# Attention block on one core: VectorE's order in the projections, the place of the x loads, and when the second head pair gets its position terms

## The chip, the core and the metric

The kernel runs on one core of a Trainium2 chip. The metric is the device time of one execution in microseconds (us). The core has a matrix engine (TensorE, PE in the profile; its weight loads are PEld), two engines for elementwise work (VectorE, DVE; ScalarE, ACT), GpSimd (POOL) and SyncE (SP), which in this kernel issues most DMA transfers. Each engine works through its own list of instructions in order and waits on semaphores for the others. Matrix products land in PSUM, a small memory[...]; operands lie in SBUF.

## The reference, cut to what matters

Eight images of 512 channels and 32 x 32 pixels, all in float32:

```python
def cbs(x, w, p, pad): return silu(bn_eval(conv2d(x, w, pad), p))

def bot_attention(x, qkv_w, rw, rh):          # 4 heads of 64, 1024 pixels
    q, k, v = split(conv2d(x, qkv_w, 0))
    r = rw + rh                                # position terms, by column and by row
    logits = einsum('bhdi,bhdj->bhij', q, k + r) * HD ** -0.5
    return einsum('bhij,bhdj->bhdi', softmax(logits), v)

t = cbs(group_norm(x), cv1_w, cv1_bn, 0)       # 512 -> 512, 1x1
ys = [t[:, :256], t[:, 256:]]
for i in range(2):                             # two bottleneck units
    z = cbs(ys[-1], m_cv1_w[i], m_cv1_bn[i], 1)        # 3x3, 256 -> 256
    z = bot_attention(z, m_qkv_w[i], m_rw[i], m_rh[i])
    ys.append(ys[-1] + silu(bn_eval(conv2d(z, m_cv2_w[i], 0), m_cv2_bn[i])))
out = x + cbs(concatenate(ys, 1), cv2_w, cv2_bn, 0)    # 1024 -> 512, 1x1
```

## The kernel before, in words

Images go one after the other; `b` counts them from 0. An image has two units, `n` = 0 and 1. In each, TensorE's work comes in this order: the 3x3 convolution, the projections to q, k and v, attention, and the 1x1 convolution `m2` (lines 887 to 902). First convolutions of the next image (`cv1`) or parts of the output convolution (`strassen`, line 933) are put between.

The program is traced in this order, and a planner then lays out each engine's list. It takes instructions by their place in the program among those that it reckons to be ready, and it gives buffers out as it goes. `tc.issue_after(ins)` sets a bound: instructions traced in the block that run on the engine of `ins` come behind `ins` on that engine. It binds no other engine.

**The convolution (`conv3x3`, line 858).** It works on 4 x 4 output tiles in a transformed space. For each of two output halves `oc` there are three filter tiles `u` of 1 MB (three pairs of rows), and each gives 32 matmul instructions of 128 columns (line 872). ScalarE and VectorE bring each product back (`columns_out`, `rows_out`, lines 405 to 439); ScalarE applies silu. `rows_out` has two parts: `first`, when two of the three products are there, and `last`.

**Loads.** All large tiles of weights share a ring of five buffers of 1 MB: filters (`load_u`, line 309), the combined projection weights `sq` (`load_sq`, line 232), `w1` (line 115) and the output convolution's weights. From image 1 on, `u_of(n)` takes the first three filters as loaded earlier, loads the second three when the second half is traced, and then `sq`. The next image's x (four tiles of 512 KB, line 104) is loaded in the program after the first convolution; its buffers are those in which the output convolution of the image before keeps its results until they are stored (line 979). All these loads stand in SP's queue, each one behind what was queued before it. Stores and residual loads of the output convolution stand in POOL's queue.

**The projections (`project_strassen`, line 538).** In image 0 a plain form is used (`project`). In images 1 to 7, both units, z is seen as a 2 x 2 block matrix, channel half by pixel half, and seven block products stand in for eight. Each of them is a q, a k and a v part. PSUM has three buffers `ps_big` of two banks and one `ps_av` of two banks; the seven products go through them as `ps_a` to `ps_e`, `ps_w` and `ps_v`. VectorE forms the operand sums `t1` to `t4` (lines 582 and 591 to 593) and the results:

| Lines | What VectorE computes |
| --- | --- |
| 606, 607 | `u` = product c + product a (q and k, then v) |
| 608, 577, 578 | `k1` of the first channel half, then its position terms (`add_r(0, 1)`) |
| 610, 611 | `v1` and `q1` |
| 616 to 618 | `k2`, `q2`, `v2` from product d |
| 621 to 623 | `k3`, `q3`, `v3` |
| 624 to 626 | product e taken from `v2`, `k2`, `q2` |
| 577, 578, twice each | position terms of the second channel half (`add_r(1, half)`) |

Line 624 reads the bank `ps_v`, and lines 625 and 626 read `ps_e`; the buffers are free for attention after that. `t`, `u` and `m5` lie in the three SBUF buffers `pt`, which the convolution's input tiles use before and attention's exponentials use after.

**Attention (`attention_fast`, line 631).** There are four groups: a pair of heads (a channel half `c`) by a half of the 512-pixel query columns. A group has eight key blocks, taken two at a time: four pairs of steps per group, 16 per unit. In each pair TensorE computes two tiles of logits (line 656), ScalarE the exponentials into `pt` (line 660), VectorE adds them to `acc` for the softmax sum (lines 666 and 668), and TensorE multiplies with v one pair behind (line 682, into the single `ps_av` buffer). At a group's end ScalarE and VectorE move the result to `ao` (lines 689 and 690), after which the next group may use `ps_av`; TensorE sums `acc` over partitions (`s_ps`, line 700). The order of trace is in the loop at line 763: `behind.get(g)` hangs other work on the groups. In the first unit of all images but the last, that work is the next image's group normalisation: statistics of two x tiles (line 444) in the first group and of two in the second, then the rest, then `cv1`. In the second unit it is loads, and products of the output convolution behind the fourth group.

Of the kernel before, what the change touches and what calls it, by code (L numbers as in the profile page):

```python
# [47 lines left out]
ALU = mybir.AluOpType  # L48
# [13 lines left out]
def kernel(  # L62
# [16 lines left out]
    nc = tc.nc  # L79
    B, C1, HW = x.shape  # L80
    C2 = out.shape[1]
    N, C = m_cv1_w.shape[:2]
    F = m_rw.shape[2]
    NX = C1 // P
    NM = C // P
# [143 lines left out]

    def load_sq(n):  # L230
        w = ring([P, 4, 3, P], "sq")
        nc.sync.dma_start(w, sq_dram[n])
        return w

# [70 lines left out]
    def load_u(n, oc, i):  # L307
        u = new_u("u")
        nc.sync.dma_start(u, u_dram[n][oc][i])
        return u  # L310
# [13 lines left out]
    def stages(act, small, ps_big, ps_av, n_pt):  # L324
# [89 lines left out]
        def rows_out(dst, r12, r34, ends):  # L414


            sd = act.tile([P, 2, 2, NT * F], F32, tag="acc", name="sd", bufs=2)
            s_, d_, big_s, big_d = sd[:, 0, 0], sd[:, 0, 1], sd[:, 1, 0], sd[:, 1, 1]
            stt, tt = nc.vector.scalar_tensor_tensor, nc.vector.tensor_tensor

            def tiles(ap):
                return ap.rearrange("p (t w) -> p t w", w=F)

            def to(r):
                return dst.rearrange("p (t r w) -> p r t w", r=4, w=F)[:, r]

            def first():
                for i, rr in enumerate((r12, r34)):
                    tt(sd[:, i, 0], rr[:, 0], rr[:, 1], ALU.add)
                    tt(sd[:, i, 1], rr[:, 0], rr[:, 1], ALU.subtract)  # L430
                stt(to(1), tiles(big_d), -0.5, tiles(d_), ALU.mult, ALU.add)
                tt(to(2), tiles(s_), tiles(big_s), ALU.subtract)

            def last():
                stt(ends, ends, -6.0, sd[:, 0], ALU.mult, ALU.add)
                stt(to(0), tiles(big_s), -0.25, tiles(ends[:, 0]), ALU.mult, ALU.add)
                stt(to(3), tiles(big_d), -2.0, tiles(ends[:, 1]), ALU.mult, ALU.add)  # L437

            return first, last
# [95 lines left out]
                qk(c)  # L535
            return q, kr, vT

        def project_strassen(n, z, sq):


            q = act.tile([P, NM, HW], F32, tag="q", name="q")
# [28 lines left out]
            def v_of(ap):  # L570
                return ap.rearrange("p (j o) -> p j o", o=P)
# [7 lines left out]

            t = act.tile([P, 4, HALF], F32, tag="pt", name="t_z", bufs=n_pt)  # L580
            t1, t2, t3, t4 = (t[:, i] for i in range(4))
            tt(t1, b12, b11, ALU.subtract)
            ps_a, ps_b, ps_v = big(), big(), ps_av.tile([P, 2, HALF], F32, tag="av", name="pv_ps")
            u, m5 = kept("u_z"), kept("m5_z")
            product(ps_a, ps_v[:, 0], block_qkv(n, 0, 0), b11)
# [21 lines left out]
            tt(u[:, 2], ps_w[:, 0], u[:, 2], ALU.add)  # L607
            tt(k1, k1, u[:, 1], ALU.add)
            add_r(0, 1)
            tt(v1, v1, v_of(u[:, 2]), ALU.add)  # L610
            tt(q1, q1, u[:, 0], ALU.add)
            ps_d = big()
            product(ps_d, ps_w[:, 1], s3, t3)
            q2, k2, v2 = places(1, 0)
# [6 lines left out]
            tt(k3, k2, m5[:, 1], ALU.add)  # L621
            tt(q3, q2, m5[:, 0], ALU.add)
            tt(v3, v2, v_of(m5[:, 2]), ALU.add)
            tt(v2, v2, v_of(ps_v[:, 0]), ALU.subtract)
            tt(k2, k2, ps_e[:, 1], ALU.subtract)
            tt(q2, q2, ps_e[:, 0], ALU.subtract)  # L626
            for half in range(NH):
                add_r(1, half)
            return q, kr, vT

        def attention_fast(n, z, at, behind, sq=None):

            q, kr, vT = project(n, z) if sq is None else project_strassen(n, z, sq)
            behind.get(-1, lambda: None)()

            ao = act.tile([P, NM, HW], F32, tag="z", name="ao")
# [124 lines left out]
            for i in range(len(pairs) + 1):  # L763
                if i < len(pairs):
                    added = logits(pairs[i])
                    g, at_q = divmod(i, NQ)
                    with tc.issue_after(added.ins):
                        if at_q == NQ - 2 and g > 0:
                            rss[g - 1] = spread(g - 1, s_drams[g - 1])
                        if at_q == 0 and g > 1:  # L770
                            scale(g - 2, rss.pop(g - 2))
                if i > 0:
                    g, j0 = pairs[i - 1][0]
                    if j0 == 0 and g > 0:
                        s_drams[g - 1] = sums(g - 1)
                    times_v(pairs[i - 1])
                    if j0 == 0:
                        with tc.issue_after(added.ins):
                            behind.get(g, lambda: None)()
# [78 lines left out]
        def conv3x3(n, vs, u_of):  # L858
            z = act.tile([P, NM, HW], F32, tag="z", name="z")
            for oc in range(NM):  # L860
                us = u_of(oc)
                r = act.tile([P, 2, 2, NT * NW, 2], F32, tag="acc", name="r_mid", bufs=2)
                ends = act.tile([P, 2, NT * NW, 2], F32, tag="rs", name="r_ends", bufs=2)
                rs = (r[:, 0], r[:, 1], ends)
                flat = [a.rearrange("p r q o -> p r (q o)") for a in rs]
                first, last = rows_out(z[:, oc, :], *flat)
                for i in range(PAIRS):
                    ps = ps_big.tile([P, 2, NC, NT * NW], F32, tag="big", name="c3_ps")
                    for row in range(2):
                        for col in range(NC):  # L870
                            for k in range(NM):
                                nc.tensor.matmul(  # L872
                                    ps[:, row, col, :], us[i][:, k, row, SLOT[col], :], vs[i][:, k, row, col, :],
                                    start=(k == 0), stop=(k == NM - 1),
                                )
                    columns_out(rs[i], ps)
                    if i == 1:
                        first()
                last()
                for half in range(NH):  # L880
                    part = z[:, oc, ts(half, HALF)]
                    last_silu = silu(part, part, bn_m1[n] + oc)
            with tc.issue_after(last_silu.ins):
                table_of(AF.Exp)
            return z

        def m2(n, ao, yi, dst_of):

# [233 lines left out]
    for b in range(B):  # L1122
        more = b + 1 < B
        y1, y1n, y2 = ypad[b % 2], ypad[(b + 1) % 2], ypad[N]

        sq = {}

        def u_of(n):
            def of(oc):
                if b == 0 and oc == 1:  # L1130
                    if n == 0:
                        with tc.issue_after(last.ins):
                            for i in range(PAIRS):
                                make(n, oc, [i])
                    else:
                        for k in range(NM):
                            raws[n, oc, k] = load_raw(n, oc, k, "kv"[k])
                        with tc.issue_after(last.ins):
                            make(n, oc, [1])
                got = [us.pop((oc, i)) if (oc, i) in us else load_u(n, oc, i) for i in range(PAIRS)]  # L1140
                if b > 0 and oc == 1:
                    sq[n] = load_sq(n)
                return got

            return of


        z = s.conv3x3(0, vs, u_of(0))
        if b == 0:
            load_bottleneck(1)  # L1150
            raws[1, 0, 0] = load_raw(1, 0, 0, "y0", 2)
            raws[1, 0, 1] = load_raw(1, 0, 1, "pt", 3)
        if more:
            xs = [load_x(act, b + 1, c, NX) for c in range(NX)]


        parts = {}
# [37 lines left out]
        behind = {g: ahead for g in range(NG)} | {NG: first, NG + 1: second}  # L1195
        if b == 0:
            behind[-1] = lambda: make(1, 0, range(PAIRS))
        ao, check = s.attention_fast(0, z, b * N * NM * NH, behind, sq.get(0))
        last = s.m2(0, ao, y1, lambda oc, half: inner(y2, oc, half))
        if more:  # L1200
            s.cv1(w1, xs, nxt, y1n, Y0S)
# [5 lines left out]
        vs = s.tiles_in(y2)  # L1207
        with tc.issue_after(last.ins):
            check()
        z = s.conv3x3(1, vs, u_of(1))  # L1210
        w2 = ws = three = stored = None
        begun = {}
        if b == 0:
# [30 lines left out]
        behind = {1: ahead, NG: first, NG + 1: second}  # L1244
        if b == 0:
            behind |= {0: prepare, 2: lambda: make_sq(0), 3: lambda: make_sq(1)}
        ao, check = s.attention_fast(1, z, (b * N + 1) * NM * NH, behind, sq.get(1))
        ylast = act.tile([P, NM, HW], F32, tag="v", name="ylast")
        last = s.m2(1, ao, y2, lambda oc, half: ylast[:, oc, ts(half, HALF)])
        with tc.issue_after(last.ins):  # L1250
# [26 lines left out]
    with tc.If(held < P):  # L1277
        with ExitStack() as gs:
# [7 lines left out]
            with tc.For_i(0, B, 1) as b:  # L1286
                xts = [load_x(g_act, b, c, NX) for c in range(NX)]
                for _ in g.group_norm(xts):
                    pass
                g_y0 = g_act.tile([P, NM, HW], F32, tag="y0", name="y0")  # L1290
                g.cv1(load_w1(), xts, g_y0, ypad[0], range(2 * NM))
                yi = ypad[0]
                for n in range(N):
                    z = g.conv3x3(n, g.tiles_in(yi), lambda oc: [load_u(n, oc, i) for i in range(PAIRS)])
                    ao = g.attention_general(n, z)
                    if n + 1 < N:
                        g.m2(n, ao, yi, lambda oc, half: inner(ypad[N], oc, half))
                        yi = ypad[N]
                g_last = g_act.tile([P, NM, HW], F32, tag="v", name="ylast")
                g.m2(N - 1, ao, yi, lambda oc, half: g_last[:, oc, ts(half, HALF)])  # L1300
                g.cv2(b, load_w2(), (g_y0, ypad[0], ypad[N], g_last))
# [51 lines left out]
```

## Time and profile before

| | Before |
| --- | --- |
| Median of three runs | 2385.78 us |
| Range of the runs | 2382.54 to 2388.15 us |
| Profiled execution's own time | 2385.39 us |
| Its span in the trace | 2383.3 us |
| TensorE busy | 2326.4 us (98%) |
| VectorE busy | 1751.7 us (73%) |
| ScalarE busy | 947.7 us (40%) |
| Granted TensorE clock, mean | 0.998 |
| Bytes moved by DMA | 226.39 MB, mean 95 GB/s |

Times in the trace count from the span's start. A row of the timeline gives start, duration, engine, line, operation, output and inputs, and in brackets the idle time of the engine before it with what ended it. A row of the waits gives who waited for whom, the total in us, how often, and the longest. Matmuls are pipelined: a row's duration runs from the first start to the modelled end of the last, so that rows overlap.

### The profile page before, as it was taken

To read this page: it belongs to the slowest core of one execution; us is meant where nothing else is said; L and a number is where in the kernel's file an instruction comes from. 1 tells how busy PE (TensorE), PEld (TensorE's weight loads), DVE (VectorE), ACT (ScalarE), POOL (GpSimd) and SP (SyncE) were. 2 spreads that over 40 slices of the span, in tenths; PEclk is the share of its full clock that TensorE was granted. 3 is DMA by queue.
4 is the path that set the end of the run, shared out by engine and by line. 5 is a ranking of instruction groups with operands and counts; after the bars stand their busy time and mean duration, and the time that the engine had idled before them with its cause. 6 is when DMAs were issued, how large, how long until landed. Compare 5 with 4: busy or idle time off the path is not lost.

```text
span 2383.3 us, 36285 instructions
## 1 busy us (share of the span) xinstructions
PE 2326.4 (98%) x14794; PEld 1168.9 (49%) x14794; DVE 1751.7 (73%) x2811; ACT 947.7 (40%) x1246; POOL 88.1 (4%) x305
## 2 busy tenths in 40 slices
PE   7999999999999999999999999999999999999998
PEld 4536345363553636446364453635536354463633
DVE  8867778686786867867588676886767867676774
ACT  1442524435154352534425344252532525325252
POOL 1000010000100001000010000100001000000001
PEclk9999999999999999999999999999999999999999
DMA  7412234030430305203161120601207021160201
GB/s 250 151 52 89 94 127 170 15 129 15 165 134 12 129 15 204 97 10 129 33 224 60 39 100 32 260 29 59 80 28 261 28 82 57 37 224 15 85 10 68
DMA packets 93069, 226.39 MB, mean 95 GB/s; under 512 B 27872, under 2 KB 49312, under 8 KB 80224
## 3 DMA queue, kind: packets, MB, share of 16 engines
q1 hardware_dynamic: 81376, 174.71, 21.3%
q0 software_dynamic: 11520, 49.29, 5.3%
q8 instruction: 118, 1.93, 0.3%
q14 instruction: 55, 0.45, 0.1%
HBM read 190.41 MB, written 33.55 MB: 94 GB/s over the span
## 4 chain that ended last, share of the span: by engine, by line
PE 81%; DVE 13%; DMA 4%; issue 2%; ACT 1%; SPq 0%; POOL 0%; DVEq 0%; ACTq 0%
PE av_ps L682 16%; PE l_ps L656 14%; PE ps L344 12%; PE c_ps L872 11%; PE c L927 8%; PE c_new L927 6%; PE p_ps L556 5%; PE m_ps L893 5%; DVE acc L668 3%; PE pv_ps L560 2%; DMA u<-u 2%; DVE st L444 1%; PE s_ps L700 1%; DVE acc L666 1%; DVE u_z L606 1%
## 5 line engine op out<-in xcount | busy, mean ns | idle before, releaser
L660 ACT ACTIVATE pt<-l_ps 128x1024 f32<-128x1024 f32 x512 | 497.9, 1022 | 436.7 <-PE l_ps L656 330.1
L668 DVE TENSOR_TENSOR acc<-acc,pt 128x1024 f32<-128x1024 f32 x384 | 469.6, 1223 | 103.8 <-ACT pt L660 78.7
L656 PE MATMUL l_ps<-q,kr 64*64 64x512 f32 x4096 | 491.2, 593 | 16.3 <-DVE q L626 12.2
L682 PE MATMUL av_ps<-pt,vT 64*64 64x512 f32 x4096 | 485.8, 592 | 6.5 <-DVE ao L690 6.5
L872 PEld LDWEIGHTS c_ps<-v_in,u 128*128 128x128 f32 x2720 | 306.7, 192 | 12.6 <-issue 7.6
L872 PE MATMUL c_ps<-v_in,u 128*128 128x128 f32 x2720 | 308.1, 275 | 4.9 <-DMA u<-u 2.8
L656 PEld LDWEIGHTS l_ps<-q,kr 64*64 64x64 f32 x4096 | 151.0, 133 | 296.8 <-issue 244.3
L682 PEld LDWEIGHTS av_ps<-pt,vT 64*64 64x64 f32 x4096 | 151.8, 133 | 283.4 <-issue 228.4
L344 PE MATMUL ps<-x,w 128*128 128x512 f32 x512 | 227.2, 600 | 2.2 <-DVE x L478 2.2
L344 PEld LDWEIGHTS ps<-x,w 128*128 128x128 f32 x512 | 97.0, 192 | 130.4 <-issue 126.8
L666 DVE TENSOR_TENSOR acc<-pt 128x1024 f32<-128x1024 f32 x64 | 78.3, 1223 | 70.4 <-ACT pt L660 70.4
L408 ACT COPY m<-c_ps 128x256 f32<-128x256 f32 x96 | 35.5, 370 | 229.8 <-PE c_ps L872 199.3
L927 PE MATMUL c_new<-t_in,ws 128*128 128x512 f32 x288 | 124.6, 592 | 0.0
L893 PE MATMUL m_ps<-ao,m_sb 128*128 128x512 f32 x256 | 112.5, 592 | 0.0
L329 ACT ACTIVATE m_kept<-m_kept,bh,sh 128x512 f32<-128x512 f32 x42 | 31.9, 806 | 146.0 <-DVE m_kept L1011 86.3
L756 DVE TENSOR_TENSOR ao<-ao,rs 128x512 f32<-128x512 f32 x64 | 44.1, 689 | 60.7 <-DMA rs<-r_dram 60.0
L927 PEld LDWEIGHTS c_new<-t_in,ws 128*128 128x128 f32 x288 | 54.7, 190 | 68.9 <-issue 66.0
L329 ACT ACTIVATE t<-m_ps,bh,sh 128x512 f32<-128x512 f32 x64 | 48.1, 776 | 83.9 <-PE m_ps L893 82.5
L556 PE MATMUL p_ps<-t_z,sq 128*128 128x512 f32 x168 | 81.3, 593 | 0.0
L373 POOL MEMSET w_rows<- 128x16 f32 x96 | 12.3, 128 | 1831.9 <-PE s_ps L700 1137.8
L893 PEld LDWEIGHTS m_ps<-ao,m_sb 128*128 128x128 f32 x256 | 48.6, 190 | 61.2 <-issue 61.2
L329 ACT ACTIVATE z<-z,bh,sh 128x512 f32<-128x512 f32 x64 | 48.6, 806 | 50.9 <-DVE z L437 50.8
(223 smaller groups left out, 2698.4 us busy)
## 6 DMA issues: line engine op xcount, KB each, us to landing
u<-u SPq DMA_DIRECT2D x85, 1024.0 KB
x<-in_x_dram SPq DMA_DIRECT2D x32, 512.0 KB
x_res<-in_x_dram POOLq DMA_DIRECT2D x28, 512.0 KB, 8.9
out_dram<-m_kept POOLq DMA_DIRECT2D x28, 512.0 KB, 7.4
w<-in_cv_w_dram SPq DMA_DIRECT2D x13, 1024.0 KB
u<-u_new POOLq DMA_DIRECT2D x12, 1024.0 KB, 5.7
rs<-r_dram SPq DMA_DIRECT2D x96, 128.0 KB
ws<-s SPq DMA_DIRECT2D x24, 512.0 KB
```

The costliest lines, as they stand in the source:

```text
L329: return nc.scalar.activation(dst, src, AF.Silu, scale=sh[:, k : k + 1], bias=bh[:, k : k + 1])
L344: nc.tensor.matmul(ps[:, half, :], w_of(k), rhs_of(k, half), start=(k == begin), stop=(k == end))
L556: nc.tensor.matmul(ps[:, o, :], w[:, o, :], rhs, start=not onto, stop=True, skip_group_check=onto)
L560: nc.tensor.matmul(v[:, ts(j, P)], rhs[:, ts(j, P)], w[:, 2, :], start=j == 0 and not onto, stop=True, skip_group_check=True,)
L656: nc.tensor.matmul(ps[kh * HD : (kh + 1) * HD, hd, :], kr[r, c, o : o + HD], q[r, c, ts(half, HALF)], start=True, stop=True,)
L660: exp = nc.scalar.activation(pt[:, i], ps, AF.Exp, scale=SCALE)
L666: return nc.vector.tensor_tensor(accs[g], pt[:, 0], pt[:, 1], ALU.add)
L668: ins = nc.vector.tensor_tensor(accs[g], accs[g], pt[:, i], ALU.add)
L682: nc.tensor.matmul(avs[g][hd * HD : (hd + 1) * HD, kh, :], vT[r, j, o : o + HD], pt[r, i, hd, :], start=(j == 0), stop=(j == NJ - 1),)
L872: nc.tensor.matmul(ps[:, row, col, :], us[i][:, k, row, SLOT[col], :], vs[i][:, k, row, col, :], start=(k == 0), stop=(k == NM - 1),)
L893: nc.tensor.matmul(pss[oc][:, half, :], m2_sb[:, n, k, ts(oc, P)], ao[:, k, ts(half, HALF)], start=(k == 0), stop=(k == NM - 1),)
L927: nc.tensor.matmul(ps[:, o, :], w[:, k, ts(o, P)], rhs[part][:, c, :], start=(k == 0 and not onto), stop=(k == KB - 1), skip_group_check=onto,
```

## The change

There are three parts, all of order; no instruction is added or taken away.

1. In the projections VectorE's `t1` comes behind `mid`, the last instruction of the second half's `first()` in `rows_out`. The additions that finish `v1`, `v2` and `q1` come behind `freed`, the subtraction of line 626. The position terms of the second channel half leave the projections and become `later`, which attention traces behind the accumulation of its second pair (`i == 1`).
2. From image 1 on, the next image's four x loads come behind the load of `sq` in SP's queue.
3. To carry this, `load_sq` also returns its DMA instruction, `first()` returns its last instruction, and `conv3x3` returns `mid` beside `z`.

```diff
     def load_sq(n):
         w = ring([P, 4, 3, P], "sq")
-        nc.sync.dma_start(w, sq_dram[n])
-        return w
+        return w, nc.sync.dma_start(w, sq_dram[n])
...
                 stt(to(1), tiles(big_d), -0.5, tiles(d_), ALU.mult, ALU.add)
-                tt(to(2), tiles(s_), tiles(big_s), ALU.subtract)
+                return tt(to(2), tiles(s_), tiles(big_s), ALU.subtract)
...
-        def project_strassen(n, z, sq):
+        def project_strassen(n, z, sq, mid):
...
-            tt(t1, b12, b11, ALU.subtract)
+            with tc.issue_after(mid.ins):
+                tt(t1, b12, b11, ALU.subtract)
...
             add_r(0, 1)
-            tt(v1, v1, v_of(u[:, 2]), ALU.add)
-            tt(q1, q1, u[:, 0], ALU.add)
...
             tt(v3, v2, v_of(m5[:, 2]), ALU.add)
-            tt(v2, v2, v_of(ps_v[:, 0]), ALU.subtract)
             tt(k2, k2, ps_e[:, 1], ALU.subtract)
-            tt(q2, q2, ps_e[:, 0], ALU.subtract)
-            for half in range(NH):
-                add_r(1, half)
-            return q, kr, vT
+            freed = tt(q2, q2, ps_e[:, 0], ALU.subtract)
+            with tc.issue_after(freed.ins):
+                tt(v1, v1, v_of(u[:, 2]), ALU.add)
+                tt(v2, v2, v_of(ps_v[:, 0]), ALU.subtract)
+                tt(q1, q1, u[:, 0], ALU.add)
+
+            def later():
+                for half in range(NH):
+                    add_r(1, half)
+
+            return q, kr, vT, later
...
                     with tc.issue_after(added.ins):
                         if at_q == NQ - 2 and g > 0:
                             rss[g - 1] = spread(g - 1, s_drams[g - 1])
+                        if i == 1 and later is not None:
+                            later()
...
                     if i == 1:
-                        first()
+                        mid = first()
...
         sq = {}
+        last_load = None
...
                 if b > 0 and oc == 1:
-                    sq[n] = load_sq(n)
+                    sq[n], last_load = load_sq(n)
...
         if more:
-            xs = [load_x(act, b + 1, c, NX) for c in range(NX)]
+
+            with tc.issue_after(last_load.ins) if last_load else nullcontext():
+                xs = [load_x(act, b + 1, c, NX) for c in range(NX)]
...
-        ao, check = s.attention_fast(0, z, b * N * NM * NH, behind, sq.get(0))
+        ao, check = s.attention_fast(0, z, b * N * NM * NH, behind, sq.get(0), mid)
```

More of the change, by code (lines that the diff above doesn't have):

```diff
@@ L623, in project_strassen, with attention_fast @@
             tt(v3, v2, v_of(m5[:, 2]), ALU.add)
-            tt(v2, v2, v_of(ps_v[:, 0]), ALU.subtract)
             tt(k2, k2, ps_e[:, 1], ALU.subtract)
-            tt(q2, q2, ps_e[:, 0], ALU.subtract)
-            for half in range(NH):
-                add_r(1, half)
-            return q, kr, vT
-        def attention_fast(n, z, at, behind, sq=None):
-            q, kr, vT = project(n, z) if sq is None else project_strassen(n, z, sq)
+            freed = tt(q2, q2, ps_e[:, 0], ALU.subtract)
[7 more added lines that the diff above has]
+            return q, kr, vT, later
+        def attention_fast(n, z, at, behind, sq=None, mid=None):
+            q, kr, vT, later = (*project(n, z), None) if sq is None else project_strassen(n, z, sq, mid)
             behind.get(-1, lambda: None)()
@@ L884, in conv3x3 @@
                 table_of(AF.Exp)
-            return z
+            return z, mid
         def m2(n, ao, yi, dst_of):
@@ L1126 @@
         sq = {}
+        last_load = None
         def u_of(n):
             def of(oc):
+                nonlocal last_load
                 if b == 0 and oc == 1:
@@ L1141, in of @@
                 if b > 0 and oc == 1:
-                    sq[n] = load_sq(n)
+                    sq[n], last_load = load_sq(n)
                 return got
             return of
-        z = s.conv3x3(0, vs, u_of(0))
+        z, mid = s.conv3x3(0, vs, u_of(0))
         if b == 0:
@@ L1209 @@
             check()
-        z = s.conv3x3(1, vs, u_of(1))
+        z, mid = s.conv3x3(1, vs, u_of(1))
         w2 = ws = three = stored = None
@@ L1246 @@
             behind |= {0: prepare, 2: lambda: make_sq(0), 3: lambda: make_sq(1)}
-        ao, check = s.attention_fast(1, z, (b * N + 1) * NM * NH, behind, sq.get(1))
+        ao, check = s.attention_fast(1, z, (b * N + 1) * NM * NH, behind, sq.get(1), mid)
         ylast = act.tile([P, NM, HW], F32, tag="v", name="ylast")
@@ L1293 @@
                 for n in range(N):
-                    z = g.conv3x3(n, g.tiles_in(yi), lambda oc: [load_u(n, oc, i) for i in range(PAIRS)])
+                    z, _ = g.conv3x3(n, g.tiles_in(yi), lambda oc: [load_u(n, oc, i) for i in range(PAIRS)])
                     ao = g.attention_general(n, z)
```

## The prediction

> **What bounds the kernel now.** I read the page first (busy shares), then the waits of TensorE, then the chain of waits and the timeline around the projections of images 1 to 7 (counted from 0), which alone run the edited `project_strassen`.
>
> ```profile
> PE 2326.4 (98%) x14794; PEld 1168.9 (49%) x14794; DVE 1751.7 (73%) x2811; ACT 947.7 (40%) x1246; POOL 88.1 (4%) x305
> ...
> PE l_ps L656 <- DVE q L626: 12.2, 14, 0.9
> PE av_ps L682 <- DVE ao L690: 6.5, 11, 2.1
> ...
> PE c_ps L872 <- DMA u<-u: 2.8, 4, 1.5
> ```
>
> TensorE (PE) is busy 98% of the span at full clock, so only its few idle places can be won. Three concern this change: 14 waits for `q` of line 626 (once per Strassen projection: 7 images, two units each), waits for `ao` of line 690, and waits for the filters `u`. Matmul ends are modelled, so I measure a stall by start times: what a gap exceeds the usual spacing (0.112 us per 128-wide matmul, 0.43 per four of attention) by. The timeline of image 3's second unit:
>
> ```profile
> 1105.23 1.23 DVE L606 TENSOR_TENSOR u_z<-p_ps,u_z 128x1024 f32<-128x1024 f32 x1 [2.46 <-PE p_ps L556]
> ...
> 1111.31 1.95 PE L656 MATMUL l_ps<-q,kr 64*64 64x512 f32 x16
> ...
> 1113.55 1.09 PE L656 MATMUL l_ps<-q,kr 64*64 64x512 f32 x8 [0.29 <-ACT pt L660]
> ...
> 1114.77 0.68 DVE L626 TENSOR_TENSOR q<-q,p_ps 128x512 f32<-128x512 f32 x1
> ...
> 1115.51 1.09 PE L656 MATMUL l_ps<-q,kr 64*64 64x512 f32 x8 [0.87 <-DVE q L626]
> 1116.41 1.90 PE L682 MATMUL av_ps<-pt,vT 64*64 64x512 f32 x16
> ...
> 1128.08 1.23 DVE L666 TENSOR_TENSOR acc<-pt 128x1024 f32<-128x1024 f32 x1 [1.10 <-ACT pt L660]
> ```
>
> From 1105.23 VectorE (DVE) runs its additions without a gap. The first logits start at 1111.31 (0.17 late), the third tile waits for the first exponential (0.47), the fourth for line 626, which frees the PSUM buffer of `ps_e` (1.05). That is 1.69 us, nearly alike in all 14 projections. The last row says VectorE has caught up by 1128: it idles 1.10 us. In the first unit of images 1 to 6 it does not. There the normalisation's statistics (line 444) come on top, and the chain of waits of image 3 stays on VectorE from 969.36 to 995.31:
>
> ```profile
> 969.36 1.23 DVE u_z L606
> ...
> 993.56 1.14 DVE acc L666
> 994.70 0.61 DVE ao L690
> 995.31 0.04 issue
> 995.36 1.95 PE av_ps L682 x16
> ```
>
> So in those six places VectorE's sum, not its order, sets when TensorE goes on. Third, SP's queue beside TensorE in the same image's first unit:
>
> ```profile
> 942.09 0.33 SPq L104 DMA_DIRECT2D x<-in_x_dram  x1
> 942.50 0.52 SPq L309 DMA_DIRECT2D u<-u  x1
> 943.11 0.53 SPq L232 DMA_DIRECT2D sq<-sq  x1
> ...
> 953.27 3.81 PE L872 MATMUL c_ps<-v_in,u 128*128 128x128 f32 x32 [0.82 <-DMA u<-u]
> ```
>
> An x load that waits for an output store (942.06) holds up the last filter tile, and the products it feeds start 0.93 us late.
>
> **The change part by part.**
>
> *Late additions (14 projections).* Lines 610, 611 and 624 (`v1`, `q1`, `v2` less its product) move behind line 626. Before, 16 instructions run from line 606 to 626; now 13. Independent 128x512 additions start 0.60 us apart in the rows, so 626 ends 3 x 0.60 = 1.80 us earlier, less a loss: 608, 577 and 578 each need the one before, and lose the fillers between them. The dependent pair 577 to 578 at 1101.35 and 1102.08 stands 0.73 apart, so 2 x 0.13 = 0.25 is lost. Here a rule speaks to the sum: the Trainium skill, "VectorE: DVE Perf Modes", "The DRAIN you can't avoid", has each operation wait until the pipe is empty, semaphore or none, so that order would be free. By it the 0.25 is nothing; the row shows otherwise, and I take the row.
>
> New end of 626 in image 3's second unit: about 1114.0. TensorE then goes: first logits without the 0.17 at 1111.14; third tile still behind the first exponential, 0.5; fourth at 1114.24, no wait for 626; done at 1115.10. The first `av_ps` needs the bank that line 624 reads. Behind 626 come 610 and 624, so 624 ends near 1115.22 and `av_ps` starts at 1115.28 instead of 1116.41: 1.13 us won. Later needs have room: `v1` is read by the third pair and `q1` by the second group, 5 and 14 us later. `u_z` is now held by `q1` until about 1115.8. If the planner gives that buffer to the second pair's `pt`, its exponential waits up to 1.4 us; the pair's `av_ps` is due 3.4 us after the first, so TensorE loses nothing: zero to zero.
>
> *Position terms (`add_r(1, ...)`, 4 x 0.60 = 2.4 us per projection).* They move from before the first accumulation to behind the second pair's. They are needed 8 pairs (27 us) on. In second units the cover is VectorE's 1.10 us of idle at 1128: TensorE's 1.13 lead and the 0.25 use it up, leaving about 0.2 us of delay to `ao`, whose bank is not wanted until 1129.7. So nothing is lost, but little more could be won.
>
> *Where the 1.13 counts.* It counts in second units of images 1 to 7 and the first unit of image 7, which has no statistics: 8 x 1.13 = 9.0 us. In the first units of images 1 to 6 the same instructions stand between 969.36 and `ao`: TensorE is early at 980, and waits that much longer at 995. Gain nothing, loss the 0.25: 6 x 0.25 = 1.5 us. From both sides: 6 x 1.13 = 6.8 won if the planner gets `ao` ahead of the next group's accumulation (line 666, 1.14 us), 6 x 0.5 = 3 lost if the four position terms run as dependent pairs too. I take 1.5 lost, since the rows show the planner interleaving both halves.
>
> *t1 (line 582), behind `mid`.* At 950.32 it holds VectorE for 1.59 us of waiting. Behind line 432 it falls into the 1.53 us that VectorE idles before line 409 at 957.57, and its product is due at 959.5. Nothing; without that idle 0.6 us, still before the product.
>
> *x behind the filters (4 loads x 6 images, images 1 to 6).* They pass up to three filter loads and `sq` on SP; image 0 is not touched, image 7 has none. POOL's stores and residual loads keep their queue and share the same DMA engines, which stand at a share of 0.98 to 1.03 from 930 to 960 at some 390 GB/s. Three x loads (1.57 MB) leave the road ahead of the last filter tile: 4 us sooner, more than any stall. The late starts before the last filter block measure 0.38, 0.93, 1.08, 0.37 and 1.60 in images 1, 3, 4, 5, 6 (none in 2): 4.4 us. Image 4's is credited to `r_mid`, but no other image has that wait and its filter was issued behind three x loads, so I count it; without it, 3.3. They shift all that follows, also where VectorE bounds. `sq` now precedes the x loads and can only be earlier. Behind the x loads stand `w1` and the next unit's filters; the last x was held until 948.40 by a store anyway, so these move little. The x is wanted by line 444 at 985.7; two megabytes at 390 GB/s after 943 land by about 960. Cover: 25 us.
>
> Sum: -9.0 + 1.5 - 4.4 = -11.9 us against the profiled execution's own 2385.39 us (span 2383.3 and 2.1 around it): 2373.5. The median of the runs, 2385.78, is 0.39 above it.
>
> **The rivals.**
>
> *More:* the first units gain too, 6 x (1.13 + 0.25) = 8.3 beyond the forecast: 2365 to 2369. For it: the planner lays VectorE's order anew. Against: line 690 follows line 666 in all 14 projections before.
>
> *The release is not what holds TensorE, so the change does not do what it says:* the planner assigns PSUM buffers anew, the fourth tile then waits for an exponential or `av_ps` for line 624, and only the filters' 4.4 less the 1.5 remain: 2382.5. For it: 0.5 of the 1.69 is ScalarE's already, and line 624 leaves my sum only 0.1 us of play.
>
> *Slower, by the bank of line 624:* it is freed before anything of attention today; tied only "behind 626", it may come after `q1` and the first accumulation, which waits for the exponential at 1114.3. Then 1114.4 + 1.1 + 1.2 + 0.7 = 1117.4, and `av_ps` starts 1.04 us later than before in eight places and 0.65 in six, where the old 0.39 before `ao` absorbs a part: 12.2 - 4.4 = 7.8 lost, 2393. It decides from 0.7 us later than before: (4.8 + 4.4)/14. Against it: the three stand ahead of attention in the program, and the planner departs from that order in the rows only where an operand was not ready.
>
> **How the numbers follow.** Forecast (2371 to 2377) 0.55; more 0.17; release without gain 0.14; slower 0.12; else 0.02. About 0.2% (4.8 us) is what a measurement of this kernel can tell from no change: the first two and a little of the rest are faster, 0.74; the third is within it, 0.14; slower 0.12. Range 2366 to 2384: it takes in "more" nearly whole and the no-gain case, and leaves out the slower one.
>
> **What would show it.** Right: line 626 no longer among TensorE's waits, `av_ps` starting about 10.1 us after line 606 in second units (11.2 now); `ao` of the first group still 25.9 to 26.2 us after line 606 in first units of images 1 to 6; no wait of line 872 for `u`; the x issues after `sq` in SP's order. Wrong: `ao` there nearer than 25.5 (more), line 624 named by `av_ps` with over 1 us, or line 444 waiting for x.

## The result, and the profile after

| | Before | After |
| --- | --- | --- |
| Median of six runs, side by side | 2384.49 us | 2372.82 us |
| Range of the runs | 2381.29 to 2388.15 | 2372.56 to 2373.30 |
| Profiled execution's own time | 2385.39 us | 2373.30 us |
| Its span in the trace | 2383.3 us | 2371.5 us |

The ratio is 0.9951, with an interval of 0.9938 to 0.9964: 11.7 us faster by the medians, 12.1 by the two profiled executions. The forecast was 2373.5 us. The changed kernel also repeats more closely: its six runs lie within 0.7 us of one another, those of before within 7 us.

The changed kernel's lines are numbered differently. Line 606 is now 607, 626 is 624 (`freed`), 624 is 627, 610 is 626, 611 is 628, 656 is 661, 682 is 687, 690 is 695 and 872 is 879; the rest of attention moves by five. The kernels of the experiments shift these numbers by a few again.

The page's busy shares, and the rows of TensorE's waits that answer to those of before (who waited for whom, total us, times, longest):

```profile
PE 2320.6 (98%) x14794; PEld 1169.8 (49%) x14794; DVE 1753.1 (74%) x2811; ACT 946.3 (40%) x1246; POOL 88.2 (4%) x305
...
PE av_ps L687 <- DVE ao L695: 10.7, 11, 2.1
PE l_ps L661 <- DVE q L624: 9.1, 14, 0.7
```

The wait for the filters `u` is gone. The wait for `q` of the release is not: it still has 14 cases, and 9.1 us where there were 12.2. The wait for `ao` has grown from 6.5 to 10.7: in the six first units TensorE now comes early and waits the longer, as the forecast had it. The timeline of image 3's second unit, the one shown before:

```profile
1101.48 1.23 DVE L607 TENSOR_TENSOR u_z<-p_ps,u_z 128x1024 f32<-128x1024 f32 x1 [2.46 <-PE p_ps L556]
...
1103.22 0.68 DVE L609 TENSOR_TENSOR kr<-kr,u_z 128x512 f32<-128x512 f32 x1
1103.94 0.69 DVE L577 TENSOR_TENSOR kr<-kr,rw_sb 128x512 f32<-128x512 f32 x1
1104.55 0.69 DVE L615 TENSOR_TENSOR kr<-p_ps,u_z 128x512 f32<-128x512 f32 x1
1105.15 0.68 DVE L578 TENSOR_TENSOR kr<-kr,rh_sb 128x512 f32<-128x512 f32 x1
...
1107.48 1.95 PE L661 MATMUL l_ps<-q,kr 64*64 64x512 f32 x16
...
1109.35 0.68 DVE L624 TENSOR_TENSOR q<-q,p_ps 128x512 f32<-128x512 f32 x1
...
1110.08 1.95 PE L661 MATMUL l_ps<-q,kr 64*64 64x512 f32 x16 [0.65 <-DVE q L624]
1110.55 0.68 DVE L627 TENSOR_TENSOR vT<-vT,pv_ps 128x512 f32<-128x512 f32 x1
...
1111.85 1.90 PE L687 MATMUL av_ps<-pt,vT 64*64 64x512 f32 x16
...
1123.51 1.22 DVE L671 TENSOR_TENSOR acc<-pt 128x1024 f32<-128x1024 f32 x1 [0.35 <-ACT pt L665]
```

Count from the start of line 607 (606 before). The release ends 8.55 us in, where it had ended at 10.22. The first `av_ps` starts at 10.37 instead of 11.18. So 0.81 of the 1.67 us gained by the release reaches TensorE. The row at 1110.08 shows where the rest stays: it covers the third and the fourth tile of logits, and it is now the third that waits for the release, since the planner gave it the buffer of `ps_e`. (It can't be the operand: line 624 writes q of the second channel half, which the first group doesn't read.) By starts that tile is 0.83 us late, and the fourth not at all. The last row says VectorE's idle time before the second group's first accumulation has shrunk from 1.10 to 0.35 us.

The chain of waits in the first unit of image 3 (start, length, what):

```profile
965.70 1.22 DVE u_z L607
...
989.82 1.14 DVE acc L671
990.95 0.61 DVE ao L695
991.57 0.04 issue
991.61 1.95 PE av_ps L687 x16
```

The second group's first `av_ps` comes 25.91 us after line 607. Before it came 26.00 after (995.36 less 969.36). The chain still stays on VectorE throughout. SP's queue and the filter products of that unit, now with the x loads after `sq`:

```profile
934.84 18.59 PE L879 MATMUL c_ps<-v_in,u 128*128 128x128 f32 x165
935.59 0.32 SPq L308 DMA_DIRECT2D u<-u  x1
939.16 0.32 SPq L232 DMA_DIRECT2D sq<-sq  x1
939.52 7.46 SPq L104 DMA_DIRECT2D x<-in_x_dram  x4
```

The products run as one row of 165 matmuls, with no idle time in brackets.

**Where the 12 us came from.** In eight places (second units of images 1 to 7, first unit of image 7) the second group's `av_ps` comes 24.78 us after line 607 instead of 25.60: 8 x 0.82 = 6.6. In the first units of images 1 to 6 it is 25.91 instead of 25.99: 6 x 0.08 = 0.5. The late starts behind the filters are gone: 4.4. Together 11.5 of the 11.8 by which the spans differ.

### The profile page after: what moved, and what is told of

The parts are those of the page before. It is cut to its first block, busy times and chain, and to the rows that moved or that the text cites. A ratio compares the mean times of both kernels' runs of the same rounds, so it can differ in the third digit from the quotient of the medians.

```text
span 2371.5 us, 36277 instructions
## 1 busy us (share of the span) xinstructions
PE 2320.6 (98%) x14794; PEld 1169.8 (49%) x14794; DVE 1753.1 (74%) x2811; ACT 946.3 (40%) x1246; POOL 88.2 (4%) x305
## 4 chain that ended last, share of the span: by engine, by line
PE 82%; DVE 14%; DMA 2%; issue 1%; ACT 0%; SPq 0%; DVEq 0%; POOL 0%; ACTq 0%
PE av_ps L687 16%; PE l_ps L661 14%; PE c_ps L879 13%; PE ps L343 10%; PE c L934 8%; PE c_new L934 6%; PE p_ps L556 5%; PE m_ps L900 5%; DVE acc L673 3%; PE pv_ps L560 2%; DVE st L443 1%; PE s_ps L705 1%; DVE acc L671 1%; DVE u_z L607 1%; DVE kr L577 1%
## 5 line engine op out<-in xcount | busy, mean ns | idle before, releaser
L687 PE MATMUL av_ps<-pt,vT 64*64 64x512 f32 x4096 | 486.6, 593 | 10.7 <-DVE ao L695 10.7
L372 POOL MEMSET w_rows<- 128x16 f32 x96 | 12.2, 128 | 1821.1 <-PE s_ps L705 1127.9
```

The lines of the kernel that those rows point to most:

```text
L687: nc.tensor.matmul(avs[g][hd * HD : (hd + 1) * HD, kh, :], vT[r, j, o : o + HD], pt[r, i, hd, :], start=(j == 0), stop=(j == NJ - 1),)
```

## Experiments

The theory (A) was that three things add up: the filters' late starts, the late additions in eight places, and a sum of VectorE that holds the six first units whatever the order. The main rivals were that the late starts were not the filters' doing, that order alone does nothing, and that the second accumulation or the release itself bounds the six places. The first three runs do one part each on the kernel before, whose median beside them was 2384.44 us. `t1` behind `mid` is in none of them. The other four go on from the changed kernel; before was 2384.44 us beside the first of them (the statistics) and 2384.09 us beside the last three. The changed kernel's 2372.82 us comes from the runs of the result above.

### x behind the filters alone

```diff
-                    sq[n] = load_sq(n)
+                    sq[n], last_load = load_sq(n)
...
-            xs = [load_x(act, b + 1, c, NX) for c in range(NX)]
+            with tc.issue_after(last_load.ins) if last_load else nullcontext():
+                xs = [load_x(act, b + 1, c, NX) for c in range(NX)]
```

> The kernel before with one part of the change alone: from image 1 on, the next image's x loads stand behind sq in SP's queue. Theory A (the three parts are separate, and the x loads in front of the last filter tile cost what TensorE stood still there): the five late starts of image 1, 3, 4, 5 and 6 (4.4 us in the trace of before) are gone, the projections keep their 11.2 us from line 606 to the first av_ps, and the time falls by 4 to 5 us against the profiled execution of before (2385.4), to about 2381. If it was this queue that made the runs of before differ by 7 us, these runs lie within 1.5 us of each other. Rival B (the stores and residual loads of POOL's queue fill the DMA engines, and the x loads are only one of several): two or three of the five late starts stay, and the time falls by 1 to 2 us.

Measured: 2380.98 us (2380.25 to 2382.99), a ratio of 0.9983 [0.9974, 0.9993]: 3.5 us faster. Its waits of TensorE are otherwise those of before:

```profile
PE l_ps L655 <- DVE q L625: 12.2, 14, 0.9
...
PE av_ps L681 <- DVE ao L689: 7.0, 11, 1.9
```

All five late starts are gone, also the one of image 4 that the trace had named after `r_mid`: it too was the filter. The places of attention stand where they stood before. The ten runs now lie 2.7 us apart, where the 24 of before lie 7: this queue probably causes much of the scatter, though 1.5 was expected, and runs of so different a number say it only roughly.

### The late additions alone

```diff
-            tt(v1, v1, v_of(u[:, 2]), ALU.add)
-            tt(q1, q1, u[:, 0], ALU.add)
...
-            tt(v2, v2, v_of(ps_v[:, 0]), ALU.subtract)
...
-            tt(q2, q2, ps_e[:, 0], ALU.subtract)
+            freed = tt(q2, q2, ps_e[:, 0], ALU.subtract)
+            with tc.issue_after(freed.ins):
+                tt(v1, v1, v_of(u[:, 2]), ALU.add)
+                tt(v2, v2, v_of(ps_v[:, 0]), ALU.subtract)
+                tt(q1, q1, u[:, 0], ALU.add)
```

> The kernel before with v1, q1 and v2's subtraction behind the line that frees ps_e, alone; t1, the position terms and the x loads stay as before. Theory A (the release of ps_e sets TensorE's wait): av_ps starts 10.4 us after line 606 instead of 11.2, the second av_ps group 24.8 instead of 25.6 in the eight places without statistics (6.6 us together) and 25.9 instead of 26.0 in the six with them (0.5), so about 7 us less than before, with the late starts for u still there. Rival C (the additions win only together with the position terms, which otherwise stand in front of the first accumulations and eat the lead): the first av_ps is early, but the second group's stays at 25.3 or later, and the time falls by 3 us or less.

Measured: 2378.63 us (2376.96 to 2381.10), 0.9973 [0.9963, 0.9984]: 5.8 us faster. The eight places reach 24.78 us, exactly as in the changed kernel, so their gain is this part's alone. The six first units get worse, 26.11 us instead of 25.99, where 25.9 was expected. The timeline of image 3's first unit shows what the order costs there:

```profile
968.23 0.68 DVE L608 TENSOR_TENSOR kr<-kr,u_z 128x512 f32<-128x512 f32 x1
968.95 0.69 DVE L577 TENSOR_TENSOR kr<-kr,rw_sb 128x512 f32<-128x512 f32 x1
969.56 0.68 DVE L614 TENSOR_TENSOR kr<-p_ps,u_z 128x512 f32<-128x512 f32 x1
```

A dependent addition starts 0.72 us after the one it needs, an independent one 0.61 after. The planner filled the gap between 577 and 578 with line 614 (before: 616) and left only the one between 608 and 577 open: 0.12 us lost, as measured.

### The position terms alone

```diff
-            for half in range(NH):
-                add_r(1, half)
-            return q, kr, vT
+            def later():
+                for half in range(NH):
+                    add_r(1, half)
+
+            return q, kr, vT, later
...
+                        if i == 1 and later is not None:
+                            later()
```

> The kernel before with the position terms of the second channel half behind the second pair's accumulation, alone. Theory A (they stand behind the release of ps_e in both orders, and VectorE's sum up to ao is the same): first av_ps at 11.2 us and second group at 25.6 and 26.0 us after line 606, as before; the time moves by less than 1 us. Rival C (they hold back the first accumulations and with them the buffers of the exponentials): the second group starts 0.3 to 0.6 us earlier in all fourteen places, 4 to 8 us in all.

Measured: 2383.06 us (2379.93 to 2385.36), 0.9996 [0.9986, 1.0005]: 1.4 us less, which the interval can't tell from nothing. The trace can: the second units stand at 25.60 as before, but the first units of images 1 to 6 at 25.78, 0.21 earlier each, 1.3 in all. The timeline there, image 3:

```profile
986.46 0.64 DVE L444 BATCH_NORM_STATS2 st<-x 128x6 f32<-128x512 f32 x1
987.01 1.20 DVE L671 TENSOR_TENSOR acc<-acc,pt 128x1024 f32<-128x1024 f32 x1
988.13 0.20 DVE L445 BATCH_NORM_AGGREGATE mv<-st 128x2 f32<-128x12 f32 x1
988.32 3.89 DVE L671 TENSOR_TENSOR acc<-acc,pt 128x1024 f32<-128x1024 f32 x3
```

The same stretch before, where the terms stood ahead of the first accumulation:

```profile
987.60 0.64 DVE L444 BATCH_NORM_STATS2 st<-x 128x6 f32<-128x512 f32 x1
988.28 0.21 DVE L445 BATCH_NORM_AGGREGATE mv<-st 128x2 f32<-128x12 f32 x1
988.40 5.16 DVE L668 TENSOR_TENSOR acc<-acc,pt 128x1024 f32<-128x1024 f32 x4
```

Accumulations need one another: the next one starts 1.32 us after the one before (four of them take 5.16), while other work starts after 1.12 (988.13 less 987.01). The terms themselves go where the statistics already parted two accumulations. But with the rest moved up by them, one accumulation falls between the last statistics and their aggregate, so that three instead of four run one behind another. That saves about 0.16 us. And the aggregate no longer stands directly behind the statistics it needs, about 0.05 more. With the same instructions as before, order alone is worth 0.21 us here. So 25.99 + 0.12 - 0.21 = 25.90, and the changed kernel has 25.91.

The three parts alone give 3.5 + 5.8 + 1.4 = 10.7 us, and 11.7 together. The interval of each reaches 2.3 to 2.5 us to either side, so this is additive as far as it can be seen.

### The statistics moved away from the first group

The changed kernel, but with the next image's statistics hung on pairs 5, 9, 12 and 14 instead of on the starts of groups 1 to 4.

```diff
+                    with tc.issue_after(added.ins):
+                        hooks.get(i, lambda: None)()
...
-            next(norm, None)
+            if b == 0:
+                next(norm, None)
...
+        hooks = {i: lambda: next(norm, None) for i in (5, 9, 12, 14)} if b > 0 else {}
```

> The changed kernel with the statistics of the next image's normalisation one group later (images 1 to 6: first two tiles behind the second group's first pair, last two behind the third's, mean behind the fourth's, scaling at the second next pair). Theory A (in the first units of images 1 to 6 VectorE's sum between line 607 and ao sets TensorE, so taking 2.9 us out of it frees TensorE): ao ends at 23.9 us after line 607 there too instead of 25.9, av_ps of the second group starts at 24.8 instead of 25.9: 6 x 1.1 = 6.8 us less than the changed kernel, about 2366. Rival D (VectorE is behind all through these units, so the wait only moves to the next groups' ao or to the scaling in front of cv1): the second group starts early, but TensorE waits as much or more at a later ao or at the products of cv1, and the time is 2371 or above.

Measured: 2367.23 us (2365.93 to 2368.59), 0.9923 [0.9906, 0.994] of before, 5.6 less than the changed kernel. The timeline of image 3's first unit:

```profile
986.50 1.23 DVE L671 TENSOR_TENSOR acc<-pt 128x1024 f32<-128x1024 f32 x1 [0.35 <-ACT pt L665]
987.72 0.69 DVE L695 TENSOR_TENSOR ao<-av_ps,ao 128x512 f32<-128x512 f32 x1
...
989.25 1.95 PE L687 MATMUL av_ps<-pt,vT 64*64 64x512 f32 x16
...
991.49 0.69 DVE L443 BATCH_NORM_STATS2 st<-x 128x6 f32<-128x512 f32 x1
```

All 14 places now stand at 24.78 us, and VectorE waits for the exponential in first units as in second ones (the same 0.35). This shows that VectorE's sum, with the statistics in it, had held the six places. 6 x (25.91 - 24.78) = 6.8 was to be had, and 5.6 came by the medians. The missing 1.2 is not fully accounted for. In the profiled run the waits for the softmax scale `rs` (below) are longer: 1.28 us in image 2 and 0.95 and 0.32 in image 5, together 2.55 against 1.54 in the changed kernel's.

### The third v behind the release as well

The changed kernel, with `v3` moved behind `freed` too, so that the release comes one instruction sooner.

```diff
-            tt(v3, v2, v_of(m5[:, 2]), ALU.add)
...
             with tc.issue_after(freed.ins):
-                tt(v1, v1, v_of(u[:, 2]), ALU.add)
+                tt(v3, v2, v_of(m5[:, 2]), ALU.add)
                 tt(v2, v2, v_of(ps_v[:, 0]), ALU.subtract)
+                tt(v1, v1, v_of(u[:, 2]), ALU.add)
```

> The changed kernel with one addition more behind the line that frees ps_e: v3, which the first group doesn't read, and v2's subtraction ahead of v1 in the program. In the changed kernel the third tile of logits waits 0.83 us for that line. Theory A (the release of ps_e alone sets the start of the third tile, and VectorE's spacing of 0.60 us per addition is what the move is worth): first av_ps at 9.8 us after line 607 instead of 10.4, second av_ps group at 24.2 instead of 24.8 in the eight places without statistics, unchanged at 25.9 in the six with them: 8 x 0.56 = 4.5 us less than the changed kernel, about 2368.3. Rival E (the first exponential is next in line: its end 2.2 us after the first logits becomes what the third tile waits for): the wait for the third tile goes from 0.83 only to 0.47, and the gain is 8 x 0.36 = 2.9 us, about 2370.

Measured: 2369.46 us (2369.12 to 2369.55), 0.9938 [0.992, 0.9956]: 3.4 below the changed kernel. The timeline of image 3's second unit, where the four tiles of logits now are one row of 32:

```profile
1106.10 3.94 PE L661 MATMUL l_ps<-q,kr 64*64 64x512 f32 x32
1107.35 0.68 DVE L623 TENSOR_TENSOR q<-q,p_ps 128x512 f32<-128x512 f32 x1
...
1109.16 0.68 DVE L626 TENSOR_TENSOR vT<-vT,pv_ps 128x512 f32<-128x512 f32 x1
1109.89 1.95 PE L687 MATMUL av_ps<-pt,vT 64*64 64x512 f32 x16
```

One instruction sooner, TensorE's wait for `q` is gone from the list of waits, and the first `av_ps` comes at 9.80 instead of 10.37 in every one of the 14 places. So the release was what held TensorE in the changed kernel. It still does, a little: by starts the third tile comes at 7.99, 0.06 behind the release's end and 0.22 later than the usual spacing. And `av_ps` now starts 0.05 after line 626 (`v2`), which the planner ran behind `v1` all the same. In the eight places `av_ps` of the second group follows at 24.26 (0.52 sooner); the six first units keep 25.90, being VectorE's. 8 x 0.52 = 4.2. The two profiled spans differ by 3.9: the part ahead of image 1's projections, which the edit doesn't touch, was 1.1 shorter, and waits later were longer, that for `rs` in image 2 by 0.8 (1.51 us instead of 0.70).

### Both, and the softmax scale one pair later

Both edits together, and then, on top of them, the scaling of a finished group by `rs` (line 761) one pair later:

```diff
-                        if at_q == 0 and g > 1:
+                        if at_q == 1 and g > 1:
                             scale(g - 2, rss.pop(g - 2))
```

> The changed kernel with both: the statistics one group later, and v3 behind the line that frees ps_e. Theory A: the two add up and more, since no unit is set by VectorE's sum any more: second av_ps group at 24.2 us after line 607 in all fourteen places, 14 x 0.56 = 7.8 us less than with the later statistics alone (2367.2), about 2359.4. Rival D (VectorE, now without idle time in front of ao, is the bound in all units): ao ends later than 23.4, the second av_ps group starts at 24.5 or later, and the time is 2363 or more.

> The kernel of both, with the scaling of a finished group (line 761) one pair later, behind the move to ao that frees ps_av. In the changed kernel VectorE waits in order for the load of rs in some images and TensorE waits for the ao behind it (0.70 us in image 2, 0.84 in image 5). Theory F (this wait is the small transfers' latency, which varies from run to run): these stalls are gone, 1 to 2 us less than the kernel of both, about 2358. Rival G (the scaling fills a place where VectorE is idle anyway, and behind the first pair it delays the accumulations): no stall goes, or another appears at the next ao, and the time is the same within 1 us or longer.

Measured for both together: 2360.21 us (2359.14 to 2361.68), 0.99 [0.9883, 0.9918], with 24.26 us in all 14 places. The two edits lift each other, as the theory asks: against the changed kernel 12.6, where each alone gave 5.6 and 3.4. The third v pays in the six first units only once the statistics are out of the way.

With the scale one pair later: 2355.20 us (2353.87 to 2355.74), 0.9877 [0.9859, 0.9894]. That is 5.0 us more, where 1 to 2 were expected. The timeline of image 2 with both edits, and the scale where it was:

```profile
711.19 0.69 DVE L761 TENSOR_TENSOR ao<-ao,rs 128x512 f32<-128x512 f32 x1 [1.21 <-DMA rs<-r_dram]
711.80 0.68 DVE L695 TENSOR_TENSOR ao<-av_ps,ao 128x512 f32<-128x512 f32 x1
...
712.54 1.95 PE L687 MATMUL av_ps<-pt,vT 64*64 64x512 f32 x16 [0.96 <-DVE ao L695]
```

The same place with the scale one pair later:

```profile
707.55 0.69 DVE L695 TENSOR_TENSOR ao<-av_ps,ao 128x512 f32<-128x512 f32 x1
...
709.08 1.95 PE L687 MATMUL av_ps<-pt,vT 64*64 64x512 f32 x16
...
711.32 0.68 DVE L761 TENSOR_TENSOR ao<-ao,rs 128x512 f32<-128x512 f32 x1
```

In the first, VectorE stands in order behind a DMA, and the instruction that frees `av_ps`'s buffer stands behind it. In the second it goes first. TensorE's waits for line 695, both edits first, then with the scale later:

```profile
PE av_ps L687 <- DVE ao L695: 6.7, 7, 1.9
```

```profile
PE av_ps L687 <- DVE ao L695: 1.1, 2, 0.6
```

Stalls of 1.03, 0.72 and 0.42 us in images 2 and 5 went, and two of 1.96 and 1.79 in image 0, which the expectation had not counted; one of 1.71 came up later in image 0. That is 4.2 of the 4.3 us by which the two profiled spans differ. This version is the fastest of all: 29 us below before, 17.6 below the change.

## Why the prediction was right, point by point

- **TensorE bounds, and only its idle places can be won.** Right. Everything gained is found again as earlier starts of TensorE.
- **x behind the filters, 4.4.** Right in the profile, where all five late starts are gone, image 4's among them. Alone it measured 3.5 by medians, with an interval that holds 4.4.
- **Late additions, 8 x 1.13 = 9.0.** The places were right, all eight; the size was not: 8 x 0.82 = 6.6. The release came as forecast or better (8.55 us after line 607; the forecast of 1114.0 in the old trace was 8.8). What failed is the step "third tile still behind the first exponential, 0.5; fourth at 1114.24, no wait for 626". The planner gave the third tile the buffer of the release, so that it waits 0.83 us in place of the 0.5 forecast, and the first logits start at 6.00 after line 607, not at 5.91. The fourth tile then starts at 9.51 instead of 9.01. The forecast had put 0.18 behind the tiles for line 624, which was not needed: 0.50 - 0.18 is the 0.3 per place. Line 624 (now 627), which the working let set `av_ps`, is done 0.62 before it starts (1110.55 + 0.68 against 1111.85): it does not bind. Moving `v3` behind the release as well took 0.57 off the start of `av_ps` and left 0.22 of the 0.83. One sign that the forecast named for being right thus failed: the release is still among TensorE's waits.
- **First units of images 1 to 6, +1.5.** The mechanism was right: VectorE's sum holds them, and without the statistics all six fall to 24.78. The size had the wrong sign, -0.5 in place of +1.5 (`ao` ends at 25.85, where 25.9 to 26.2 was named as a sign). Two dependent pairs were to cost 0.25; the planner filled one of them, so 0.12 was lost. The position terms were costed at nothing and win 0.21 in these six places.
- **The row against the rule.** By order alone the late additions lost 0.12 us in each of the six places and the terms won 0.21. The Trainium skill ("VectorE: DVE Perf Modes", "The DRAIN you can't avoid") says that the next operation doesn't start until the pipe is empty; the working took from it that order costs nothing. The same section excepts a next operation that isn't held, which starts earlier, and the working left that out. Here additions of 0.68 us start 0.60 to 0.61 apart when independent and 0.72 when one needs the other. Taking the row was right, though the working applied it to the one pair that the planner fills and not to the accumulations.
- **t1, nothing.** Right, though not run alone. From the fourth group's first `av_ps` to the next `u_z` addition of line 607 it takes 80.47 us after the first units of images 1 to 6 and 100.59 after the second ones, in the changed kernel as with the x loads moved alone, where `t1` stands as before. So nothing of it reaches the path.
- **Position terms, nothing.** Right in second units (25.60 with and without), and 0.21 off in first units, as said. "Little more could be won" in second units was too dark: 0.35 us of VectorE's idle time was left, and `v3` won 0.52 more in each of the eight places.

The two misses were -2.4 us and +2.0 us and nearly cancelled. That is luck: the total is closer than its terms. Of the rivals, "more" came true in its sign alone; the release does free TensorE; the slower one would have needed line 627 behind the first accumulation, and it stands before it. The late additions alone come to their places' sum (6.6 less 6 x 0.12 is 5.9, and 5.8 was measured). What stays open: why the third v alone and the later statistics alone fall about 1 us short of theirs; the waits for `rs` vary by about that much from trace to trace.

## What to carry to other kernels

When a buffer's release is moved forward, list every tile that could be given that buffer: the gain ends at the earliest of them, not at the one that waited before. Where an engine's sum bounds a stretch, taking work out of the stretch (the statistics, 5.6 us) is worth more than reordering it (0.5 us), and `v3`'s reordering paid in all 14 places only once that was done. Put an in-order instruction that waits for a DMA behind those that free the busiest engine's buffers; one pair later was worth 5.0 us by the medians and 4.3 by the profiled spans.

## What the runs showed of the hardware beyond that

- The gap between dependent VectorE additions (starts 0.72 us apart, against 0.61 when independent, at 128x512) was not seen where an independent instruction stood between them. Nor was that between two accumulations of 128x1024 (1.32 against 1.12).
- The order of loads in one queue seems to set not only the time but its scatter. With that queue as before, the late starts in images 2 to 6 cost 4.5 us in the trace of before, 3.1 with the position terms alone and 2.2 with the late additions alone; with the x loads behind the filters, at most 0.2 in any trace. (Taken as what the time from the fourth group's first `av_ps` to the next `u_z` addition exceeds 100.59 by.) The runs of before lie 7 us apart, with the x loads behind the filters 2.7, with the late additions or the position terms alone 4.1 and 5.4, with all three 0.7. The four kernels built on the changed one lie 0.4 to 2.7 apart, so the 0.7 of six runs need not be a property of the change.
- What TensorE waits for `rs` from DRAM varies from trace to trace. In the eight kernels that scale at the old place it was 0.7 to 1.5 us in image 2; in image 5 it was nothing in three of them and 0.7 to 1.0 in the other five (both at the third group of the first unit).
